# A two-layer trunk on one core: the first layer's feed-forward by pairs of chunks and seven block products, its inner width in two parts, and the keys' and queries' weights loaded by blocks

## The chip, the core and the metric

The kernel runs on one core of one Trainium2 chip. A core has a matmul engine (TensorE, "PE" in the profile), a vector engine (VectorE, "DVE"), a scalar engine (ScalarE, "ACT"), a general engine (GpSimd, "POOL") and a sync engine (SyncE, "SP") that here only starts transfers (DMAs). The engines run side by side. Each executes its own instructions in a fixed order and waits on semaphores where it needs another's result. The metric is the device time of one execution, in microseconds (us); lower is better.

## The reference

Two layers run on `x` of shape 4 x 512 x 512 (batch, tokens, width). Both branches of a layer read the same layer-normed rows:

```python
xn = _layernorm(x)
x = x + L0_attn(xn) + L0_ffn(xn)
xn = _layernorm(x)
x = x + L1_attn(xn) + L1_ffn(xn)
```

The first layer's attention is a scan. Each of 32 heads carries a 16 x 16 matrix `W1` and a bias `b1`, and goes through the 512 tokens in 32 steps of 16 tokens:

```python
def step(carry, x):
    W1_s, b1_s = carry
    xq, xk, xv, eta_mb = x
    Z1 = xk @ W1_s + b1_s
    grad = _ln_fused_l2_bwd(Z1, xv - xk, ln_w, ln_b)
    Attn1 = jnp.tril(xq @ xk.swapaxes(-1, -2))
    b1_bar = b1_s - jnp.tril(eta_mb) @ grad
    Z1_bar = xq @ W1_s - eta_mb * Attn1 @ grad + b1_bar
    last_eta = eta_mb[:, :, -1, :, None]
    W1_new = W1_s - (last_eta * xk).swapaxes(-1, -2) @ grad
    b1_new = b1_s - jnp.sum(last_eta * grad, axis=-2, keepdims=True)
    out = xq + _ln(Z1_bar, ln_w, ln_b)
    return ((W1_new, b1_new), out)
```

So a step can't begin before the step ahead of it has its gradient. The scan's output is normed again and multiplied by `o_w`.

The first layer's feed-forward has an inner width of 1408 (11 blocks of 128):

```python
g = jnp.einsum('th,ih->ti', xf, gate_w) * gate_s
u = jnp.einsum('th,ih->ti', xf, up_w) * up_s
hdn = jax.nn.silu(g) * u
out = jnp.einsum('ti,hi->th', hdn, down_w) * down_s
```

The second layer is an attention of 16 heads on low-rank latents, and a feed-forward with four experts. Everything is in 32-bit floats.

## The kernel before

**Chunks.** The first layer works on 8 chunks `ch` of 4 scan steps (64 tokens of each of the 4 batches, 256 columns). For a chunk, `norm_rows` loads and norms the rows and `norm_turn` (L154) turns them on PE into `xT`, 128 partitions by 4 blocks of the width by 256 columns. `keys` and `queries` (through `features`, L242) make `k1` and `q1` from `xT` with the weights `wk` and `wq`, which are loaded whole at the start (L163, L188) and stay on the chip. `token_tile` (L258) makes, for 128 tokens, a tile `rows` with keys, targets and learning rates, and stores it to memory by 8 small stores from SP (L294).

**The scan.** For step `n`, `prepare` (L303) loads `kv` and lays out `sk`, `km` and the query part of `wq_bd` on POOL. `first_product` (L338) is a matmul group into `pz`. `gradient` (L353 to L390) is a chain of small DVE and ACT operations on 128 x 256 elements from `pz` to `grad`. `update` (L393) copies `grad` into `g_bd` (two copies on DVE, two on ACT) and adds 16 products to the state `wacc`, which stays in PSUM. `weights_out` (L327) copies the new state to `wq_bd`, for the next `pz`. `out_operands` (L417, with `gh` on POOL, L421) and `emit_out` (L433) give the step's output in `pso`.

**Filler.** Between the parts of a step, the program calls `fill(us)`. It takes pieces from a generator `between(ch)` (L656) until the estimated lengths that the pieces yield add up to what is due: 11, 3 and 8 us in a step. `between(ch)` holds the feed-forward of chunk `ch` (`gate_up`, L465, eleven times, then `down`, L481, for each half of the chunk), the projections of the next chunk, and `finish` (L545) of the chunk before. `finish` is the norm of the scan's output, the product with `wo`, the sum of the layer and the norm for the next layer. It is itself a chain over PE, ACT and DVE: squares (`pn_sq`) into a product with `bones`, roots (`pn_rs`), a product with `onesd` for the means, another for the variances, then `wo`. The last chunks also do `latents` (L620 on), the first products of the second layer, from rows that are stored and read back (`latent_rows`).

**A gate/up block.** `gate_up(ch, i)` loads two 256 KB blocks, `wg` and `wu` (two buffers each, from SP), multiplies each with `xT` (four products of 128 x 128 by 256 columns each) into the two halves of one PSUM bank `pf` (two banks), and makes `hid` by a silu on ACT (`sg`) and one DVE operation (L478). `down` loads 11 blocks `wd` of 256 KB (four buffers, from SP) for each half of a chunk and adds 11 products of 512 columns into `pd`.

**Order.** The calls above are not the final order. The framework's planner puts the instructions of the program into one fixed order for each engine before it runs, from its own estimates of their costs and from what each needs; the queue of SP is one of these orders, and a transfer that waits for a buffer holds up those behind it. The pools give each tile name a number of buffers: a tile waits until the reader of the tile that had its buffer is done.

**Layer 1** follows from L800 on. Its four-expert feed-forward (L933 to L1018) already multiplies by seven block products where eight would be the plain way, with sums of its operands on DVE and with the partial results held on ACT. The change doesn't touch it.

Of the kernel before, what the change touches and what calls it, by code (L numbers as in the profile page):

```python
# [42 lines left out]
NI = INTER // P  # L43

# [11 lines left out]
def trunk_kernel(ctx: ExitStack, tc: tile.TileContext, a: dict, out: bass.AP):  # L56
# [49 lines left out]
    with ExitStack() as px:  # L106
# [16 lines left out]
        xTs, xns = {}, {}  # L123
# [30 lines left out]
        def norm_turn(ch):  # L154
            xTs[ch] = wk.tile([P, NC, CW], F32, tag="xT", name=f"xT{ch}", bufs=3)
            for u in range(2):
                nc.scalar.copy(xTs[ch][:, :, u * P : (u + 1) * P], transposed(xns.pop((ch, u))))
                yield 0.6
# [4 lines left out]
        wk_w = load(one, "wk", [P, NC, HS], a["wk"].rearrange("(c p) o -> p c o", p=P))  # L163
# [24 lines left out]
        wq_w = load(one, "wq", [P, NC, HS], a["wq"].rearrange("(c p) o -> p c o", p=P))  # L188
# [53 lines left out]
        def features(ch, w, got, tag, bufs):  # L242

            t = got[ch] = wk.tile([P, NC, CW], F32, tag=tag, name=f"{tag}_{ch}", bufs=bufs)
            for be in range(NC):
                pp = psum()[:, :CW]
                for c in range(NC):
                    mm(pp, w[:, c, be * P : (be + 1) * P], xTs[ch][:, c, :], c == 0, c == NC - 1)
                nc.scalar.copy(t[:, be, :], pp)
                yield 1.72  # L250

        def keys(ch):
            return features(ch, wk_w, k1, "k1", 2)

        def queries(ch):
            return features(ch, wq_w, q1, "q1", 3)
# [46 lines left out]
        def prepare(n):  # L303

            ch, i = divmod(n, CH)
            kv = wk.tile([P, B, RW], F32, tag="kv", name=f"kv_{n}", bufs=3)
# [158 lines left out]
        def gate_up(ch, i):  # L465
            if i == 0:
                hid[ch] = wk.tile([P, NI, CW], F32, tag="hid", name=f"hid_{ch}", bufs=1)
            pf = ps_ff.tile([P, 2, CW], F32, tag="pf", name=f"pf_{ch}_{i}")
            for j, nm in enumerate(("wg", "wu")):
                w = wk.tile([P, NC, P], F32, tag=nm, name=f"{nm}_{ch}_{i}")  # L470
                nc.sync.dma_start(out=w, in_=a[nm][i])
                for c in range(NC):
                    mm(pf[:, j, :], w[:, c, :], xTs[ch][:, c, :], c == 0, c == NC - 1)
            if i < 10:
                next(copies, None)
            sg = wk.tile([P, CW], F32, tag="sg", name=f"sg_{ch}_{i}")
            nc.scalar.activation(sg, pf[:, 0, :], AF.Silu, scale=gs[:, i : i + 1])  # L477
            nc.vector.scalar_tensor_tensor(  # L478
                hid[ch][:, i, :], pf[:, 1, :], us[:, i : i + 1], sg, ALU.mult, ALU.mult
            )  # L480
            yield 3.43  # L481

        def down(ch, u):
            xr = wk.tile([P, HS], F32, tag="xr", name=f"xr_{ch}_{u}")
            load_rows(xr, a["x"], ch, u)
            pd = ps_dn.tile([P, HS], F32, tag="pd", name=f"pd_{ch}_{u}")
            for i in range(NI):
                w = wk.tile([P, HS], F32, tag="wd", name=f"wd_{ch}_{u}_{i}", bufs=4)
                nc.sync.dma_start(out=w, in_=a["wd"][i * P : (i + 1) * P, :])
                mm(pd, hid[ch][:, i, u * P : (u + 1) * P], w, i == 0, i == NI - 1)  # L490
                if i in (3, 7):
                    yield 3.43
            t = wk.tile([P, HS], F32, tag="yf", name=f"yf_{ch}_{u}", bufs=4)
            nc.vector.tensor_mul(t, pd, dsc)
            nc.gpsimd.tensor_add(xr, xr, brow)
            nc.gpsimd.tensor_add(t, t, xr)
            yf[ch, u] = t
            yield 2.57
# [46 lines left out]
        def finish(ch):  # L545
# [49 lines left out]
            if ch >= NCHUNK - 2:  # L595
                t = wk.tile([P, NC, CW], F32, tag="xT", name=f"xl_{ch}", bufs=3)
                part = parts[ch] = t.rearrange("p c w -> p (c w)").rearrange("p (u c e x) -> p u c e x", u=2, c=NC, e=E)
# [10 lines left out]
        parts, lw = {}, []  # L608
# [13 lines left out]
        def latent_rows(k):  # L622
            t = parts[2 * k, 2 * k + 1] = one.tile([P, 4, NC, E, 32], F32, tag=("wk", "wv", "wq")[k], name=f"xl_{k}")
# [32 lines left out]
        def between(ch):  # L656

            fin = finish(ch - 1) if ch > 0 else iter(())
            if ch + 1 == NCHUNK:
                latent_operands()  # L660
            for i in range(NI):
                yield from gate_up(ch, i)
                if ch + 1 == NCHUNK and i in (2, 5, 8):
                    latent_rows(i // 3)
                if i == NI - 3:
                    yield from take(fin, 1)
            if ch == 0:
                yield from finish_constants()
            nxt = iter(())
            if ch + 1 < NCHUNK:  # L670
                nxt = chain(
                    norm_turn(ch + 1), keys(ch + 1), token_tile(ch + 1, 0), token_tile(ch + 1, 1), queries(ch + 1)
                )
            else:
                yield from fin
            for u in range(2):
                dn = down(ch, u)
                for j in range(3):
                    yield from take(nxt, 2)
                    yield from take(dn, 1)  # L680
                    yield from take(fin, 1)
            yield from nxt
            done.add(ch + 1)
            yield from fin
            if ch + 2 < NCHUNK:
                norm_rows(ch + 2)
            if ch + 1 == NCHUNK:
# [786 lines left out]
```

## Time and profile before

The three runs before took 2028.45, 2035.72 and 2035.77 us; the median is 2035.72. The profile is of one more execution.

| what | value |
|---|---|
| profiled execution, its own time | 2030.29 us |
| its span in the trace | 2028.3 us |
| granted clock of PE, mean | 0.998 |
| PE busy, whole span | 1968.2 us |
| layer 0 (until the first product of layer 1, `epg`) | 0 to 969.3 us |
| layer 1 | 969.3 to 2028.3 us |
| loads of `wg` and `wu` | 88 and 88, of 256 KB |
| loads of `wd` | 176, of 256 KB |

A group of instructions is printed as line, engine, operation, the tile written and the tiles read, shapes, count, busy time, mean duration in ns, and then the idle time of the engine ahead of them with what ended it. `L117` is the helper that records every matmul of layer 0, so these are told apart by their tiles. One product in 32-bit floats shows as two matmul records. The timeline gives one line for successive instructions of a kind: start, duration, engine, line, operation, tiles, shapes, count, and in brackets the idle time before it and its releaser.

### The profile page before, as it was taken

Reading aid. Unit: us, or ns where it says so; the run is one execution under the profiler, and the core shown is the slowest. Engines: PE = TensorE matmul, PEld = TensorE weight load, DVE = VectorE, ACT = ScalarE, POOL = GpSimd, SP = SyncE. Lnnn points to the kernel's source line nnn. Section 1 sums busy time; section 2 is a strip of 40 time slices with the busy share of each in tenths; the row PEclk is TensorE's granted clock in tenths of the full one; section 3 lists DMA queues with packets and bytes.
Section 4 is the critical chain, followed back from the end, with each engine's and each line's share of the span. In section 5 each row is a group of like instructions: output and inputs, shape, how many; then the busy total and the mean of one; then the engine's idle time right before and its main releaser. Section 6 shows DMA issues by size and latency. Waiting matters only on the chain.

```text
span 2028.3 us, 30787 instructions
## 1 busy us (share of the span) xinstructions
PE 1968.2 (97%) x10502; PEld 1245.2 (61%) x10502; DVE 1302.3 (64%) x2720; ACT 863.2 (43%) x1763; POOL 631.8 (31%) x707
## 2 busy tenths in 40 slices
PE   8999999999999999998999999999999999999999
PEld 6777676767676776744776445555555555555555
DVE  4546657575756574754654487777777777777773
ACT  2233343333343443422322365555555555555552
POOL 4334242434342433421001132223223232354320
PEclk9999999999999999999999999999999999999999
DMA  6757576646373655545831144344434443333332
GB/s 166 210 129 220 132 193 166 183 128 184 114 203 116 179 151 163 182 136 189 281 104 56 39 101 117 95 103 115 108 94 114 103 114 86 97 97 89 94 100 93
DMA packets 318472, 270.90 MB, mean 134 GB/s; under 512 B 87660, under 2 KB 239405, under 8 KB 317677
## 3 DMA queue, kind: packets, MB, share of 16 engines
q1 hardware_dynamic: 298080, 237.31, 43.2%
q0 software_dynamic: 8736, 26.31, 4.5%
q10 hardware_dynamic: 11500, 5.32, 0.9%
q8 instruction: 84, 1.38, 0.3%
q14 instruction: 72, 0.58, 0.1%
HBM read 174.18 MB, written 34.87 MB: 103 GB/s over the span
## 4 chain that ended last, share of the span: by engine, by line
PE 47%; DVE 1%; SPq 1%; ACT 1%; issue 0%; DMA 0%; DVEq 0%; ACTq 0%
PE sc L1134 9%; PE pc L1202 9%; PE pq L1124 7%; PE px L1245 5%; PE p L1245 4%; PE epg L969 3%; PE epo L1032 3%; PE pk L1116 2%; PE epu L969 1%; SPq L1194 1%; PE po L1302 1%; PE pw L868 1%; PE pvo L886 1%; ACT prob L1139 1%; ACT prob L1144 0%
## 5 line engine op out<-in xcount | busy, mean ns | idle before, releaser
L1139 ACT ACTIVATE prob<-sc,mx 128x512 f32<-128x512 f32 x256 | 174.3, 683 | 164.2 <-DVE mx L1136 159.4
L1134 PE MATMUL sc<-kT,qT 96*128 96x512 f32 x512 | 230.6, 592 | 1.6 <-DVE prT_head L1183 1.3
L1202 PE MATMUL pc<-prT,lv 128*128 128x512 f32 x488 | 219.6, 593 | 1.2 <-DMA prT<-tt 1.2
L1109 POOL TENSOR_TENSOR kT<-t_k,t_k 32x512 f32<-32x512 f32 x64 | 80.6, 1259 | 407.6 <-PE pq L1124 235.6
L1163 DVE STREAM_TRANSPOSE tt<-prob 128x512 f32<-128x512 f32 x248 | 170.3, 706 | 55.2 <-ACT prob L1144 43.7
L117 PE MATMUL pf<-xT,wg 128*128 128x256 f32 x704 | 173.7, 388 | 5.3 <-DMA wg<-in_wg 2.7
L1144 ACT ACTIVATE prob<-prob,sm 128x512 f32<-128x512 f32 x256 | 176.5, 713 | 0.0
L1124 PE MATMUL pq<-cq,uq 128*128 128x512 f32 x384 | 175.3, 592 | 0.8 <-ACT ctxT L1204 0.8
L1134 PEld LDWEIGHTS sc<-kT,qT 96*128 96x128 f32 x512 | 96.8, 190 | 124.1 <-issue 118.9
L1136 DVE TENSOR_REDUCE mx<-sc 128x1 f32<-128x512 f32 x256 | 168.0, 677 | 2.3 <-PE sc L1134 0.3
L117 PE MATMUL pf<-xT,wu 128*128 128x256 f32 x704 | 167.0, 380 | 1.3 <-DMA wu<-in_wu 1.3
L117 PE MATMUL pd<-wd,hid 128*128 128x512 f32 x352 | 165.9, 600 | 1.8 <-DMA wd<-in_wd 1.7
L117 PEld LDWEIGHTS pf<-xT,wg 128*128 128x128 f32 x704 | 132.1, 192 | 32.9 <-issue 7.6
L1202 PEld LDWEIGHTS pc<-prT,lv 128*128 128x128 f32 x488 | 92.5, 190 | 93.7 <-issue 90.7
L117 PEld LDWEIGHTS pf<-xT,wu 128*128 128x128 f32 x704 | 133.7, 190 | 20.4 <-DMA wu<-in_wu 2.3
L478 DVE SCALAR_TENSOR_TENSOR hid<-pf,us,sg 128x256 f32<-128x256 f32 x88 | 41.9, 477 | 153.9 <-ACT sg L477 153.5
L1124 PEld LDWEIGHTS pq<-cq,uq 128*128 128x128 f32 x384 | 72.8, 190 | 93.1 <-issue 81.5
L314 POOL TENSOR_SCALAR sk<-k,m 128x256 f32<-128x256 f32 x64 | 61.1, 964 | 179.8 <-PE pz L117 167.7
L421 POOL TENSOR_SCALAR gh<-grad,m 128x256 f32<-128x256 f32 x64 | 61.2, 967 | 153.2 <-DVE grad L390 135.5
L117 PEld LDWEIGHTS pd<-wd,hid 128*128 128x128 f32 x352 | 63.4, 190 | 60.5 <-issue 45.2
L1109 POOL TENSOR_TENSOR qT<-t_q,t_q 32x512 f32<-32x512 f32 x64 | 80.6, 1260 | 56.7 <-DVE t_q L1105 56.6
L477 ACT ACTIVATE sg<-pf,gs 128x256 f32<-128x256 f32 x88 | 41.5, 473 | 132.9 <-PE pf L117 132.5
(304 smaller groups left out, 3546.6 us busy)
## 6 DMA issues: line engine op xcount, KB each, us to landing
prT<-tt SPq DMA_DIRECT2D x992, 64.0 KB, 2.0
wd<-in_wd SPq DMA_DIRECT2D x176, 256.0 KB, 3.0
wg<-in_wg SPq DMA_DIRECT2D x88, 256.0 KB, 3.1
wu<-in_wu SPq DMA_DIRECT2D x88, 256.0 KB, 3.1
cq<-lat_d SPq DMA_DIRECT2D x48, 256.0 KB, 4.3
rows<-rows SPq DMA_DIRECT2D x128, 66.0 KB, 2.2
kv<-rows POOLq DMA_DIRECT2D x32, 264.0 KB, 4.1
gu<-in_gu SPq DMA_DIRECT2D x3, 2048.0 KB, 8.8
```

The source lines that it names most:

```text
L117: nc.tensor.matmul(out, lhsT=lhsT, rhs=rhs, start=start, stop=stop, skip_group_check=True)
L421: nc.gpsimd.tensor_scalar_mul(gh[:, :, h, :], g, m2[:, h : h + 1])
L969: nc.tensor.matmul(ps, lhsT=w[:, c, :], rhs=x[:, c], start=start and c == 0, stop=c == 1, skip_group_check=True)
L1109: nc.gpsimd.tensor_sub(t[RD:mid, :], t1[RD:mid, :], t2[RD:mid, :])
L1124: nc.tensor.matmul(pq, lhsT=w[f"uq{i}"][:, h, :], rhs=cqs[hg, b][:, i, :], start=(i == 0), stop=(i == nq - 1))
L1134: pin(nc.tensor.matmul(ps, lhsT=qT[:KQ, i * P : (i + 1) * P], rhs=kT[:KQ, :], start=True, stop=True))
L1136: pin(nc.vector.tensor_reduce(mx, ps, AX.X, ALU.max, negate=True))
L1139: pin(nc.scalar.activation(pr, ps, AF.Exp, bias=mx, scale=1.0, accum_out=sm))
L1144: pin(nc.scalar.mul(pr, pr, sm))
L1163: nc.vector.transpose(out=tt[:, :, :, i, :], in_=pr.rearrange("p (kb e j) -> p kb e j", e=2, j=K))
L1202: pin(nc.tensor.matmul(pc, lhsT=lv[:, b, k, :], rhs=prT[:, k, :], start=(k == 0), stop=(k == E - 1)))
L1245: nc.tensor.matmul(ps[:, q, :], lhsT=a[:, k, q * P : (q + 1) * P], rhs=w[:, k, :], start=start and k == 0 and q == 0, stop=k == 1, skip_gr ...
```

## The change

The first layer's feed-forward is done for a pair `k` of chunks instead of one chunk. `xT` holds both chunks of the pair. For an inner block `i`, the weights of gate and up make a 2 x 2 block matrix (gate and up, by two halves of the width 512), and the pair's `xT` another (two halves of the width, by two chunks). Their product is formed from seven block products (each two matmuls of 128 x 128 by 256 columns) instead of eight. The sums of the right-hand operand are four DVE subtractions for each pair (`right_sums`), those of the left-hand operand four POOL operations for each pair and block, one block ahead (`left_sums`). Four ACT copies and four DVE additions for each pair and block put the products together. Both `pf` banks serve one block.

`hid` holds six inner blocks of both chunks. The inner width is done in two parts, blocks 0 to 5 and 6 to 10: `down` is called twice for each half of a chunk, the first part's sums are copied from `pd` to `yf` by ACT, the second part's are added by DVE.

To make room, `wk` and `wq` no longer stay on the chip: for each chunk the four 128-wide blocks of each are loaded into the buffers of `wg` and `wu` (the first chunk's keys use `wk` loaded whole into `hid`'s buffer). `kv`, `xT` and `q1` go from three buffers to two. `between` has a new order for even and odd chunks, and the rows and the order of the latents are placed differently.

```diff
         def norm_turn(ch):
-            xTs[ch] = wk.tile([P, NC, CW], F32, tag="xT", name=f"xT{ch}", bufs=3)
+            if ch % 2 == 0:
+                xTp[ch // 2] = wk.tile([P, NC, 2, CW], F32, tag="xT", name=f"xT{ch}")
+            xTs[ch] = xTp[ch // 2][:, :, ch % 2, :]
...
-        wk_w = load(one, "wk", [P, NC, HS], a["wk"].rearrange("(c p) o -> p c o", p=P))
+        wk_w = wk.tile([P, FF_FIRST, 2, CW], F32, tag="hid", name="wk", bufs=1)
+        wk_w = wk_w[:, :NC].rearrange("p c h t -> p c (h t)")
+        nc.sync.dma_start(out=wk_w, in_=a["wk"].rearrange("(c p) o -> p c o", p=P))
...
-        wq_w = load(one, "wq", [P, NC, HS], a["wq"].rearrange("(c p) o -> p c o", p=P))
...
+        def blocks_of(nm, ch):
+            def block(be):
+                w = wk.tile([P, NC, P], F32, tag="wu" if be % 2 else "wg", name=f"{nm}_{ch}_{be}")
+                nc.sync.dma_start(
+                    out=w, in_=a[nm].rearrange("(c p) o -> p c o", p=P)[:, :, be * P : (be + 1) * P]
+                )
+                return w
+            return block
...
-            kv = wk.tile([P, B, RW], F32, tag="kv", name=f"kv_{n}", bufs=3)
+            kv = wk.tile([P, B, RW], F32, tag="kv", name=f"kv_{n}")
...
-        def gate_up(ch, i):
-            if i == 0:
-                hid[ch] = wk.tile([P, NI, CW], F32, tag="hid", name=f"hid_{ch}", bufs=1)
-            pf = ps_ff.tile([P, 2, CW], F32, tag="pf", name=f"pf_{ch}_{i}")
-            for j, nm in enumerate(("wg", "wu")):
-                w = wk.tile([P, NC, P], F32, tag=nm, name=f"{nm}_{ch}_{i}")
-                nc.sync.dma_start(out=w, in_=a[nm][i])
-                for c in range(NC):
-                    mm(pf[:, j, :], w[:, c, :], xTs[ch][:, c, :], c == 0, c == NC - 1)
...
+        def right_sums(k):
+            b11, b12, b21, b22 = (xTp[k][:, 2 * c : 2 * c + 2, h, :] for c in range(2) for h in range(2))
+            t = wk.tile([P, 4, 2, CW], F32, tag="t_sums", name=f"t_sums_{k}", bufs=1)
+            t1, t2, t3, t4 = (t[:, n] for n in range(4))
+            nc.vector.tensor_sub(t1, b12, b11)
+            nc.vector.tensor_sub(t2, b22, t1)
+            nc.vector.tensor_sub(t3, b22, b12)
+            nc.vector.tensor_sub(t4, b21, t2)
...
+        def left_sums(k, i):
+            a11, a12, a21, a22 = (w[:, 2 * c : 2 * c + 2, :] for w in lefts[k, i] for c in range(2))
+            t = wk.tile([P, 3, 2, P], F32, tag="s_sums", name=f"s_sums_{k}_{i}")
+            s1, s2, s4 = (t[:, n] for n in range(3))
+            nc.gpsimd.tensor_add(s1, a21, a22)
+            nc.gpsimd.tensor_sub(s2, s1, a11)
+            nc.gpsimd.tensor_sub(a21, a11, a21)
+            nc.gpsimd.tensor_sub(s4, a12, s2)
...
+        def gate_up(k, i):
...
+            pa = ps_ff.tile([P, 2, CW], F32, tag="pf", name=f"pfa_{k}_{i}")
+            pb = ps_ff.tile([P, 2, CW], F32, tag="pf", name=f"pfb_{k}_{i}")
+            g = wk.tile([P, 2, CW], F32, tag="cg", name=f"cg_{k}_{i}")
+            up = wk.tile([P, 2, CW], F32, tag="cu", name=f"cu_{k}_{i}", bufs=1)
+            x = pa[:, 0]
...
+            product(x, o["a11"], r["b11"], True)
+            nc.scalar.copy(g[:, 0], x)
+            product(pa[:, 1], o["a12"], r["b21"])
+            product(x, o["s2"], r["t2"])
+            nc.scalar.copy(g[:, 1], x)
+            product(pb[:, 0], o["s1"], r["t1"], True)
+            nc.scalar.copy(up[:, 1], pb[:, 0])
+            nc.vector.tensor_add(g[:, 0], pa[:, 1], g[:, 0])
             yield 3.43
+            if more:
+                left_sums(k, i + 1)
+            product(x, o["s3"], r["t3"])
+            nc.scalar.copy(up[:, 0], x)
+            product(pb[:, 0], o["s4"], r["b22"])
+            nc.vector.tensor_add(g[:, 1], pb[:, 0], g[:, 1])
+            nc.scalar.activation(g, g, AF.Silu, scale=gs[:, i : i + 1])
+            product(pb[:, 1], o["a22"], r["t4"])
+            nc.vector.tensor_add(up[:, 1], up[:, 1], up[:, 0])
+            nc.vector.tensor_add(up[:, 0], pb[:, 1], up[:, 0])
+            nc.vector.scalar_tensor_tensor(hid[k][:, n], up, us[:, i : i + 1], g, ALU.mult, ALU.mult)
+            yield 2.6
...
+        def down(ch, u, part):
...
+            parts_i = range(FF_FIRST, NI) if part else range(FF_FIRST)
...
+            if part:
+                t = yf[ch, u]
+                nc.vector.tensor_add(t, pd, t)
+                nc.vector.tensor_mul(t, t, dsc)
...
+            else:
+                t = yf[ch, u] = wk.tile([P, HS], F32, tag="yf", name=f"yf_{ch}_{u}", bufs=4)
+                nc.scalar.copy(t, pd)
...
+            if not odd:
+                yield from norm_turn(ch + 1)
+                right_sums(k)
+                for i in range(FF_FIRST):
+                    yield from gate_up(k, i)
...
+                for c in range(2):
+                    for u in range(2):
+                        if c and u:
+                            ahead(k, FF_FIRST)
+                        yield from down(ch + c, u, 0)
+                return
...
+            for i in range(FF_FIRST, NI):
+                yield from gate_up(k, i)
...
+            yield from down(ch - 1, 0, 1)
+            yield from down(ch - 1, 1, 1)
...
+                latent_rows(2)
+                for key in ((0, 1), (2, 3), 6, (4, 5)):
                     yield from latents(key)
```

## The prediction

> **What bounds the kernel now.** I read first the busy time of each engine and the forty slices, where the last layer-0 slices and the first are the ones to look at.
>
> ```profile
> PE 1968.2 (97%) x10502; PEld 1245.2 (61%) x10502; DVE 1302.3 (64%) x2720; ACT 863.2 (43%) x1763; POOL 631.8 (31%) x707
> ...
> PE   8999999999999999998999999999999999999999
> ```
>
> The matmul engine sets the time: 1968.2 of 2028.3 us. Next I cut the span into stretches (columns: stretch and length, then PE, weight loads, DVE, ACT and POOL busy, clock, DMA share, GB/s).
>
> ```profile
> 885.00:969.30 84.30, 75.88 (x324) 39.95 (x315) 37.28 (x88) 17.36 (x53) 15.11 (x24) 1.00 0.52 163
> 969.30:2028.30 1059.00, 1045.76 (x3200) 590.40 (x3199) 729.11 (x1366) 518.26 (x1082) 282.08 (x232) 1.00 0.40 104
> ```
>
> Layer 1 takes the last 1059 us. Only layer 0, the first 969.3 us, is touched. There PE is idle 46.1 us (969.3 less its busy time 923.3). So a shorter PE program is worth its whole length only where PE still has work to put behind the other waits. The timeline of PE shows those waits at the scan (columns: start, duration, engine, line, operation, count, idle before and releaser):
>
> ```profile
> 251.82 1.08 PE L117 MATMUL pz<-wq_bd,sk 128*32 128x128 f32 x32
> ...
> 257.27 1.89 PE L117 MATMUL pf<-xT,wg 128*128 128x256 f32 x8
> 258.99 1.89 PE L117 MATMUL pf<-xT,wu 128*128 128x256 f32 x8
> 263.60 0.48 PE L117 MATMUL pso<-a_bd,gh 128*32 128x68 f32 x17 [2.72 <-POOL gh L421]
> ...
> 264.69 0.70 PE L117 MATMUL pz<-gsum,bones 128*128 128x256 f32 x2
> 266.78 1.08 PE L117 MATMUL pz<-wq_bd,sk 128*32 128x128 f32 x32 [1.40 <-ACT wq_bd L332]
> ```
>
> Each of 32 scan steps runs pz on PE, then the gradient on DVE and ACT, then wacc on PE, then copies to wq_bd for the next pz. PE fills the gradient with feed-forward and projection matmuls. Summed over the stage, waits of that chain cost PE 14.5 us: g_bd 5.4, gh 5.6, wq_bd 2.5, bias_o 1.0. The feed-forward rows show the pitch: starts 257.27 and 258.99 are 1.72 apart for 4 products of 128x128 by 256 columns (two records each), 0.43 us a product.
>
> **How long the gradient is.** From DVE's timeline of a quiet step, number 11, whose pz with wq_bd began at 354.47:
>
> ```profile
> 355.62 0.42 DVE L356 TENSOR_REDUCE s<-pz 128x16 f32<-128x256 f32 x1 [0.89 <-PE pz L117]
> ...
> 363.37 0.88 DVE L395 COPY g_bd<-grad 32x256 f32<-32x256 f32 x2
> ```
>
> The first operation starts at 355.62 and g_bd is whole at 364.25: 8.6 us (8.5 to 8.9 in other quiet steps). With 0.3 from pz's end and 0.1 to wacc, PE needs 9.2 us of other work between pz and wacc; steps with other DVE work took 10 to 17. Behind wacc, wq_bd takes 2.0 us.
>
> **Part 1, two products fewer in sixteen.** Each of 44 gate/up blocks (4 pairs, 11 inner blocks) runs 7 block products of two instead of 8: 44 x 2 = 88 products x 0.4325 = **-38.0 us**. Left-hand and right-hand sums go to POOL and DVE, extra copies to ACT: POOL 176 sums of 128x256, half of this row each:
>
> ```profile
> L1235 POOL TENSOR_TENSOR s_ops<-ctxT 128x512 f32<-128x512 f32 x15 | 19.4, 1293 | 83.3 <-ACT ctxT L1204 83.3
> ```
>
> That is 0.65 x 176 = 114 us; DVE about +87 (44 blocks of four operations at 0.42 and one at 0.75 for two at 0.48, plus 16 right sums and 16 additions at 0.69); ACT about +60 us. None of the three comes near PE's total, so PE covers it everywhere outside the gradient; where that cover is missing it lengthens the chain, priced below.
>
> **Part 2, coupling inside a block.** Four products reuse one bank while ACT copies it out, both pf buffers are held by one block, and the cu buffer is single. Before shows no such block in layer 0; layer 1's seven-product feed-forward, epg, has the same shape and runs with hardly a stall (PE idle in all of layer 1: 1059 - 1046 = 13 us). That bounds it at 0 from below; above, two exposed 0.37 us copies a block, 44 x 0.8 = 35. Nearest is the epg row, but there nothing else asks ACT and DVE; I take 0.2 a block, **+9**.
>
> Here a rule is weighed. The rows first:
>
> ```profile
> L374 DVE TENSOR_TENSOR pair<-xh,by_tok x32: 361/424/1430, 54.2 to 889.5; 128x256 f32<-128x256 f32 x32
> L390 DVE TENSOR_TENSOR grad<-u,rl x32: 360/425/1304, 59.3 to 892.9; 128x256 f32<-128x256 f32 x32
> ```
>
> Minimum, median, maximum in ns: a two-input DVE operation takes 424 and at worst three times that. The Trainium skill, GPSIMD Engine Reference, Key points, says that GpSimd's SBUF interfaces are shared with VectorE and contend with DVE instructions that have two SBUF inputs. That speaks against the change: POOL's 114 us of sums are 13% of 900 us, and 7 such operations in 32 steps are 224, so about 28 collisions of 0.4 us = 11 us, half of them on the path (estimate): **+5**. By the rows' medians alone it would be 0. I take the 5; together **+14**, range 0 to 40.
>
> **Part 3, what PE has to do during the gradient.** The changed kernel's built order of instructions (it holds no times) gives the products between each pz and its wacc; I cost them by the rows above (plus 4.5%, by which layer 0's busy time exceeds my sum). Before never has under 7.5 us there. After has 4.3 in step 2, 4.2 in 7, 5.1 in 10, 1.5 in 11, 4.7 in 15, 0.6 in 19, 4.0 in 23, 0.6 in 27. The cause is in the queue: keys' and queries' weights now come as 60 loads of 256 KB on SP, into the buffers of wg and wu, so each waits there for PE to release a buffer, and down's wd loads (four buffers) stand behind them and behind the sixteen stores of rows, which wait for the token tile:
>
> ```profile
> 29.64 8.28 SPq L294 DMA_DIRECT2D rows<-rows  x16
> ...
> wd<-in_wd SPq DMA_DIRECT2D x176, 256.0 KB, 3.0
> ```
>
> 16 issues take 8.28 us, 0.52 each. So the built order puts the downs, which would have filled the gradient, behind the next wacc. Shortfalls against 9.2: 4.9 + 5.0 + 4.1 + 7.7 + 4.5 + 8.6 + 5.2 + 8.6 = 48.6, and 4.8 for other DVE operations that the order puts inside four of these gradients: 53.4. Ten other steps fall short by 0.4 to 2.9, together 12. In steps 2, 10, 19 and 23 the next pz follows wacc after 1.1 us of work where 2.0 are needed: 3.6. In three of them the products on gh come before wacc, and gh on POOL is ready about 1 us after g_bd: 3. Sum 72; before's own 14.5 go, as these waits stand in the new order's count: **+57.5**. Range: 40 (the eight alone, less 14) to 75 (busy gradients of 11).
>
> **Part 4, the tail of layer 0.** After the last step the finishing of the last chunk is a chain, of which PE covers a part:
>
> ```profile
> 922.07 1.99 PE L117 MATMUL pj<-pn_sq,bones 128*128 128x512 f32 x4 [2.88 <-ACT pn_sq L549]
> ...
> 939.71 0.59 PE L117 MATMUL pj<-pn_sq,onesd 128*128 128x256 f32 x2
> ...
> 946.37 0.50 PE L117 MATMUL pj<-onesd,pn_sq 128*128 128x1 f32 x4
> ```
>
> Behind the last wacc, before has 62.9 us of PE work and after 42, since the latents move earlier. Squares to means took 17.6 us (922.07 to 939.71), of which I count 13 for the DVE and ACT chain: after has 5.4 us of work there (7.7 short); means to variances needs 4.7 and has 0.5 (4.2); about 3 at the transposes; 15, less about 4 of before's 7.3 that go: **+11**, range 0 to 15. The 2 MB gu load now waits for the last q1 addition, with xe behind it; I find it landing 5 us ahead of its use, so 0.
>
> **Part 5, start.** The whole wq load (1 MB) is gone, but its blocks 2 and 3 queue behind the first 16 row stores: queries end near 46 us instead of 39.5, the first pz comes at the same time (47.6) with 4 us less filler behind PE: **+4**, range -2 to 8. Loads of wg and wu halve (176 to 88) and 60 new ones come, 3 us each to land behind PE's fill; a late one is bounded by the 4.0 us that PE waited for wg and wu before, and I take 0.
>
> **Edits at nothing.** kv goes from three buffers to two: its load lands in 4.1 us and its buffer is free after the step before, with whole steps (13.4 us the shortest, pz 251.29 to 264.69) between; uncovered it costs 4.1 a step. q1 and xT lose a buffer, and hid holds six blocks for two chunks: in the built order their last readers come well before the next writer; uncovered, each is one chunk's wait of a few us. On POOL four sums of 0.65 stand among sk, km and gh; one ahead of gh delays it 0.65, part of the 3 above.
>
> **Sum.** 2030.3 (the profiled execution: span 2028.3 and 2 outside) - 38.0 + 14 + 57.5 + 11 + 4 = 2078.8; I say **2079**. The runs shown are 1.8 below to 5.5 above that execution, their median 2035.7.
>
> **Rivals.** (a) *Blocks bound by ACT, DVE and the shared port.* ACT's silu, four copies and table switches stand in one queue. For it: single cu, no second pair of banks. Against: epg. At 35 us plus 1.5 us in ten more gradients, part 2 is 50: 2079 + 36 = 2115. (b) *The tail and the coupling are covered.* Parts 2 and 4 at 0: 2079 - 25 = 2054; with the smaller shortfalls of part 3 at 0 too, 2042. For it: epg; against: DVE's doubled work per block. (c) *The other side: the gradient is shorter when nothing stands beside it.* In the eight starved steps its place is DVE's sequence from pz to g_bd; each us less there saves 8. Not slower (2036) needs 2079 - 2036 = 43, so 9.2 must fall to about 3.8 there. Against: DVE's fifteen operations of the chain in the quiet step sum to 6.6 us by themselves, and 7.0 would give 2079 - 18 = 2061; so this rival keeps little chance, and that mostly where parts 2 and 4 come out low too. (d) *The change doesn't do what it says*: the built order has 88 products fewer, so no.
>
> **How the numbers follow.** As forecast 0.64, own range 2058 to 2098 (parts 2 to 5 at a mixture of their ends); (a) 0.17; (b) 0.13; (c) 0.06. Half a per cent, 10 us, is about what a measurement of this kernel can tell from no change. Below 2025.5 lies 0.05, most of (c); within, (b)'s lower half and the rest of (c), 0.09; slower 0.86. Leaving out half of (a) above 2115 and most of (c), the range is 2042 to 2115.
>
> **What the profile after would show.** PE busy near 1930 us; pf products 1232 instead of 1408 records; PE waits on g_bd of 4 to 9 us in steps 2, 7, 10, 11, 15, 19, 23 and 27, some 60 us in all; layer 1 unchanged at 1059; first epg near 1018. Part 2 is right if waits in the blocks sum to some 10 us and pair or grad stay near 424 ns in the median. The prediction fails if the starved gradients take far less than 9 us, or PE reaches those pz late, or if pf stalls are tens of us.

## The result and the profile after

The changed kernel takes 2174.7 us (median of 4 runs, 2172.35 to 2175.98) against 2035.5 us before: a ratio of 1.069, 95% interval 1.068 to 1.071. It is slower, as forecast, but by 139 us where 43 were forecast, and far above the 2115 at which the prediction's range ended.

The busy times and the forty slices of the profile after:

```profile
PE 1999.3 (92%) x10326; PEld 1230.3 (57%) x10326; DVE 1407.3 (65%) x2884; ACT 921.5 (42%) x1908; POOL 771.5 (36%) x883
...
PE   7989888788898969899789999999999999999999
...
PEclk9999999999999989999889999999999999999999
```

PE has 176 records fewer (88 products), and yet is busy 31 us longer. DVE, ACT and POOL grew by 105, 58 and 140 us, where the prediction had 87, 60 and 114. The PE row has dips through the whole first half. The clock row has dips that were not there before. The stretches (length, then busy times, clock, DMA share, GB/s) place it:

```profile
47.70:1040.00 992.30, 865.19 (x6833) 582.87 (x6832) 629.08 (x1409) 380.70 (x767) 448.14 (x584) 0.95 0.48 134
1040.00:1109.30 69.30, 50.18 (x171) 28.56 (x170) 25.08 (x54) 11.59 (x34) 12.08 (x21) 0.83 0.54 175
1109.30:2172.30 1063.00, 1047.50 (x3200) 591.35 (x3198) 729.95 (x1366) 518.15 (x1082) 281.69 (x232) 1.00 0.40 103
```

Layer 0 now ends at 1109.3 instead of 969.3. Layer 1 takes 1063 instead of 1059. In layer 0 PE's granted clock was 0.95 and, at the end, 0.83. What PE waited for in layer 0 (engine, line, releaser: total us, times, longest):

```profile
PE pso L119 <- POOL gh L440: 25.8, 7, 7.7
PE pfb L119 <- POOL s_sums L512: 18.3, 2, 9.4
PE wacc L119 <- ACT g_bd L414: 17.0, 3, 8.3
PE pj L119 <- DVE pn_sq L625: 16.5, 4, 8.7
PE pd L119 <- DMA wd<-in_wd: 8.8, 10, 2.0
PE wacc L119 <- DVE g_bd L414: 8.3, 1, 8.3
PE pz L119 <- DVE gsum L425: 7.7, 1, 7.7
PE pfa L119 <- DVE cg L544: 7.6, 4, 2.9
```

I split layer 0 of each kernel in the same way. From stretches of 1 us I add PE's busy time, its idle time, and busy time x (1 - granted clock), which is what PE lost to a lower clock; busy time less that loss is the work at full clock.

| kernel | end of layer 0 | PE idle | lost to the clock | busy at full clock |
|---|---|---|---|---|
| before | 969.3 | 46.9 | 3.3 | 919.1 |
| after | 1109.3 | 157.5 | 41.8 | 910.0 |
| before, weights by blocks (f1) | 1033.8 | 87.4 | 27.9 | 918.5 |
| after, eight products (f2) | 1058.3 | 108.5 | 26.1 | 923.7 |
| after, merged stores (g1) | 1061.7 | 111.1 | 39.2 | 911.4 |
| the same, eight products (g2) | 1005.9 | 69.3 | 11.7 | 924.9 |
| f1 with merged stores (g3) | 982.9 | 52.2 | 8.3 | 922.4 |
| before, merged stores (g4) | 965.9 | 43.8 | 3.4 | 918.6 |
| g1, no left sums, no copies (h3) | 1007.8 | 88.5 | 24.7 | 894.6 |

After against before: idle +110.6, clock +38.5, work at full clock -9.1, layer 1 +4: 144 us, the difference of the two spans (2172.3 - 2028.3).

### The profile page after: what moved, and what is told of

Read it like the earlier page. It is cut to its first block, busy times and chain, and to the rows that moved or that the text cites. A ratio compares the mean times of both kernels' runs of the same rounds, so it can differ in the third digit from the quotient of the medians.

```text
span 2172.3 us, 31148 instructions
## 1 busy us (share of the span) xinstructions
PE 1999.3 (92%) x10326; PEld 1230.3 (57%) x10326; DVE 1407.3 (65%) x2884; ACT 921.5 (42%) x1908; POOL 771.5 (36%) x883
## 3 DMA queue, kind: packets, MB, share of 16 engines
q1 hardware_dynamic: 316560, 228.92, 39.2%
## 4 chain that ended last, share of the span: by engine, by line
PE 74%; DVE 13%; DMA 4%; ACT 3%; issue 2%; POOL 2%; SPq 1%; ACTq 0%; DVEq 0%; POOLq 0%
PE pj L119 12%; PE sc L1260 9%; PE pc L1328 9%; PE pq L1250 7%; PE pfa L119 5%; PE px L1371 5%; PE pd L119 4%; PE pfb L119 4%; PE p L1371 4%; PE epg L1095 3%; PE epo L1158 3%; PE pk L1242 2%; PE pz L119 2%; PE epu L1095 1%; DMA wd<-in_wd 1%
## 5 line engine op out<-in xcount | busy, mean ns | idle before, releaser
L119 PE MATMUL pd<-wd,hid 128*128 128x512 f32 x352 | 178.8, 626 | 20.4 <-DMA wd<-in_wd 8.8
L119 PE MATMUL pfa<-xT,wg 128*128 128x256 f32 x352 | 95.2, 393 | 3.6 <-ACT cg L538 3.1
L1254 ACT ACTIVATE qT<-pq,b_UQ 64x512 f32<-64x512 f32 x64 | 43.6, 682 | 110.0 <-PE pq L1250 110.0
L544 DVE TENSOR_TENSOR cg<-pfa,cg 128x256 f32<-128x256 f32 x44 | 18.2, 414 | 109.8 <-ACT cg L541 109.3
L340 POOL TENSOR_SCALAR km<-kv,m2n 128x256 f32<-128x256 f32 x64 | 62.8, 992 | 74.8 <-PE wacc L119 62.6
L1225 DVE SCALAR_TENSOR_TENSOR t_k<-pk,b_UK,trig_k 32x512 f32<-32x512 f32 x64 | 47.9, 748 | 63.1 <-ACT kT L1243 63.0
L1225 DVE SCALAR_TENSOR_TENSOR t_q<-pq,b_UQ,trig_q 32x512 f32<-32x512 f32 x64 | 47.9, 748 | 60.1 <-ACT qT L1254 58.5
```

The lines of the kernel that those rows point to most:

```text
L119: nc.tensor.matmul(out, lhsT=lhsT, rhs=rhs, start=start, stop=stop, skip_group_check=True)
L1225: nc.vector.scalar_tensor_tensor(t1[RD:mid, :], ps[RD:mid, :], bias[RD:mid, :], trig[RD:mid, :], ALU.add, ALU.mult)
```

## The experiments

Theory A said that the starved gradients come from SyncE's queue; B, from the blocks of keys' and queries' weights; C, that an idle spell costs clock afterwards; D, that the seven products' coupling costs. Before took 2033 to 2035.5 us (medians) beside each set of runs.

**e1, the stores of rows from ScalarE's queue.**

```diff
-                    nc.sync.dma_start(
+                    nc.scalar.dma_start(
                         out=rows_d[ch][i, ...
```

> The changed kernel with one edit: the 128 stores of rows are started from ScalarE's queue instead of SyncE's. Theory A (in SyncE's queue the wd loads stand behind the rows stores, so the built order has no feed-forward for the gradients at the ends of chunks): PE's work between pz and wacc, by the built order, is 8.1 us or more in every step instead of 0.6 to 5.1 in eight of them, so the waits of 5 to 9 us in the scan go (about 70 us of idle time) and with them some ten spells of half clock at 2 us each: about 2085 us (2065 to 2105). Theory B (the wd loads stand behind the blocks of keys' and queries' weights): nothing changes, 2174. If idle spells have no price of their own beside their length: about 2105.

2184.2 us, ratio 1.075 (1.072 to 1.078): a little slower than the changed kernel. The built order did have 8 us or more of PE work in every gradient, yet idle time was 161.7 us. The view of the tile `rows` tells why (count: minimum, median, maximum ns; then who waited for it, in us and times):

```profile
L313 ACTq DMA_DIRECT2D rows<-rows x128: 309/441/2427, 32.3 to 926.4; - x128
...
  ACT q L255: 50.8, 6
  ACT rows L289: 25.9, 5
  ACT rows L309: 15.2, 5
```

The 128 issues, at a median of 0.44 us, and the waits of the stores themselves held ScalarE: behind them the copies of queries alone waited 50.8 us. The edit put a new wait in the place of the old one; it neither supports nor refutes A.

**e2, the block loads from ScalarE's queue.**

```diff
-                nc.sync.dma_start(
+                nc.scalar.dma_start(
                     out=w, in_=a[nm].rearrange("(c p) o -> p c o", p=P)[:, :, be * P : (be + 1) * P]
```

> The changed kernel with one edit: the 60 block loads of wk and wq are started from ScalarE's queue instead of SyncE's. Theory A: the starved steps stay, 2170 to 2180. Theory B: they go, about 2085 to 2105.

2175.0 us, one run: unchanged, and in its profile PE idles between pz and wacc as long in the starved steps as in the changed kernel's (8.4 us in steps 11 and 27). The queue of the block loads is not what starves the gradients.

**e3 and i1, zero products in the starved steps.**

```diff
+        idle_w = one.tile([P, 32], F32, tag="idle_w", name="idle_w")
+        nc.gpsimd.memset(idle_w, 0.0)
+        extra = {2: 14, 7: 12, 10: 14, 11: 18, 15: 14, 19: 20, 23: 14, 27: 20}
         def update(n, g, pre):
+            for _ in range(extra.get(n, 0)):
+                mm(wacc[:32].rearrange("p b be d -> p (b be d)"), idle_w, wvl[:, 0, :CW], False, True)
```

> The changed kernel with 126 added products of a zero weight tile (128 rows by 32 columns) with 256 columns, added into the state, in the eight starved steps only (12 to 20 a step): 54 us of PE work that changes no value. Theory C (an idle spell of PE over 3 us halves its clock, and each such spell costs 2 us more afterwards): idle time of layer 0 falls by about 55 us, about ten of 21 half-clock spells go, and the kernel is faster by 15 to 20 us, 2155 to 2160, with more work. If the clock has no part in it: the gradient chain sets the time in these steps and the kernel stays at 2174, or it is slower where a step's products last longer than its chain, up to 2185.

2169.0 us (2166.6 to 2174.3), 6 us below the changed kernel with 54 us more of PE work. In its profile idle time is 110.8 us (-47) and the loss to the clock 25.2 (-16.6), as C has it; busy time grew by 39, and the sum is -8. The whole gain is under half of what C foretold, and the runs of the two kernels overlap. i1 has 91 such products instead of 126:

> As the run with zero products (126 of them, 54 us of work, 2169 us; its profile had 39 us more busy time, 47 us less idle time and 17 us less lost to the half clock than the changed kernel), with 91 of them (39 us), so that no step's work outlasts its gradient chain. Theory C (an idle spell has a price after it): the zero products only take the place of idle time, and the spells they end leave 10 to 16 us: 2158 to 2164. If the clock's price is nothing: 2174.

2186.1 us (2175.5 to 2190.9): slower than the changed kernel, against both numbers. Its built order differs elsewhere too; idle time fell only to 131.1 and the loss to the clock stayed at 41.8, with a wait of 8.8 us in another step (3). So the clock's price is seen in the traces, but no run isolates it as a total, and every edit brings another planned order with it.

**f1, weights by blocks alone, on the kernel before.**

```diff
-        wq_w = load(one, "wq", [P, NC, HS], a["wq"].rearrange("(c p) o -> p c o", p=P))
...
-                    mm(pp, w[:, c, be * P : (be + 1) * P], xTs[ch][:, c, :], c == 0, c == NC - 1)
+                    mm(pp, wb[:, c, :], xTs[ch][:, c, :], c == 0, c == NC - 1)
```

> The kernel before with one part of the change alone: keys' and queries' weights by blocks (60 loads into the buffers of wg and wu, the first keys' weights whole in hid's buffer), everything else as before, eight products. If blocks starve the gradients by themselves: by its built order PE has 0.6, 2.3 and 2.5 us of work between pz and wacc in steps 3, 7 and 28, short by 8.6, 6.9 and 6.7 us, with three half-clock spells of 2 us and 4 us at the start: +32, about 2066. If the loads are hidden: 2035.

2095.3 us, ratio 1.031 (1.027 to 1.034): +62, where +32 was expected. This one part costs almost half of the loss. Its timeline in step 3, PE first and then SyncE's queue:

```profile
147.68 0.63 PE L117 MATMUL pso<-wq_bd,wh 128*32 128x64 f32 x32
158.35 0.32 PE L117 MATMUL pso<-a_bd,gh 128*32 128x68 f32 x1 [10.05 <-POOL gh L434]
...
162.10 2.86 PE L117 MATMUL pf<-xT,wg 128*128 128x256 f32 x8
```

```profile
142.17 0.37 SPq L484 DMA_DIRECT2D wg<-in_wg  x1
142.64 0.38 SPq L484 DMA_DIRECT2D wu<-in_wu  x1
143.53 0.33 SPq L484 DMA_DIRECT2D wg<-in_wg  x1
```

PE sits idle for 10 us (148.3 to 158.4) and only behind the update of the state takes a gate product. Its `wg` block had been started at 143.53 at the latest and taken 3.2 us to land. The load was in time. It is PE's fixed order, made from the planner's estimates, that has the product behind the gradient. The price is beyond the step as well: 162.10 to 164.80 is 2.7 us for a group that takes 1.72 at full clock.

**f2, eight products in the changed kernel.**

```diff
-            product(x, o["a11"], r["b11"], True)
-            nc.scalar.copy(g[:, 0], x)
...
+            for ps, wb, half in ((pa, w[0], False), (pb, w[1], True)):
+                for h in range(2):
+                    for c in range(NC):
+                        mm(ps[:, h], wb[:, c, :], xTp[k][:, c, h, :], c == 0, c == NC - 1)
...
```

> The changed kernel with eight block products for seven and no sums, copies or additions of products; pairs, two parts, weights by blocks and the order of the pieces stay. If the seven products cost more by their coupling than they take off PE, as between the two runs with the rows stores on ScalarE (66 us): 2105 to 2115. If that was peculiar to those two: 38 us of work more and nothing gained, 2190 to 2210.

2112.5 us, ratio 1.039 (1.036 to 1.043). With more PE work the kernel is 62 us faster: seven products cost 62 us here. Pairs, two parts and the new order cost 17 beyond f1. The steps from before to f1, to f2 and to after (62 + 17 + 62 = 141) make up the whole loss. e4, the same in e1's frame, agrees (2118.3 against 2184.2):

> As the run with the rows stores on ScalarE's queue, and with eight block products in place of seven: pairs of chunks, inner width in two parts and the weights by blocks stay, the sums of operands and the copies and additions of products are gone. If the 88 products taken out are worth their 38 us: 38 us above that run. If the split into products in two banks with copies gives most of that back, as PE's records of layer 0 suggest (29 us more busy time at full clock than 88 products fewer would leave): 5 to 15 us above it. If the coupling costs more than it brings: below it.

**f3 and f4, the left-hand sums.** f3 makes all four on VectorE (the first is shown), f4 leaves them out.

```diff
-            nc.gpsimd.tensor_add(s1, a21, a22)
+            nc.vector.tensor_add(s1, a21, a22)
...
```

> The changed kernel with the left-hand sums on VectorE instead of GpSimd. If the sums are late because they stand in GpSimd's queue behind the load of kv and km (18.3 us of waits on s_sums in two steps, with two half-clock spells): 2150 to 2160. If these steps are starved whoever makes the sums: 2170 to 2185, with the waits under another name.

> The changed kernel without the left-hand sums (seven products of the plain weight blocks, so the gated products are other numbers): the products, copies, additions and order stay. If GpSimd's 176 sums and the shared interface are what costs: down by 30 us or more, to 2140 or less. If the coupling through PSUM, the copies and the starved gradients are: 2160 to 2175.

f3: 2162.3 us, between its two cases; the waits of 9.8 and 8.2 us in steps 7 and 15 stay under VectorE's name. f4: 2150.1 us, also between its cases: the sums cost 25 us.

**g1 to g4, 32 stores of rows instead of 128, on the same queue.**

```diff
-        rows_d = [dram.tile([CH, NS, K, B, RW], ...
+        rows_d = [dram.tile([CH, K, NS, B, RW], ...
-                for i in range(CH):
-                    p0 = b2 * CT + i * K
-                    nc.sync.dma_start(
-                        out=rows_d[ch][i, :, :, 2 * u + b2, :].rearrange("s t x -> t s x"), in_=t[p0 : p0 + K]
-                    )
+                nc.sync.dma_start(
+                    out=rows_d[ch][:, :, :, 2 * u + b2, :].rearrange("i t s x -> (i t) s x"),
+                    in_=t[b2 * CT : (b2 + 1) * CT],
+                )
-            nc.gpsimd.dma_start(out=kv, in_=rows_d[ch][i].rearrange("s t b x -> (s t) b x"))
+            nc.gpsimd.dma_start(out=kv, in_=rows_d[ch][i].rearrange("t s b x -> s t b x"))
```

> The changed kernel with the 128 stores of rows merged into 32, on the same queue (a store for each batch of a token tile, memory laid out by token first, kv read accordingly). Theory A, second form (the stores fill SyncE's queue in the plan, so the plan puts feed-forward behind gradients, whether its loads have landed on the chip or not): in the new built order PE has 7.5 us or more between pz and wacc in every step, so about 65 us of idle time and 20 us of half clock go: 2085 to 2100. Theory D (what costs is the coupling of products, copies and sums inside the gate/up blocks): 2150 to 2175.

2124.2 us, ratio 1.044 (1.041 to 1.047): 50 us below the changed kernel, between the numbers of the two theories (24 above A's, 26 below D's). In layer 0, PE's waits of more than 5 us fall from ten to two, and neither is in the scan. So the starved gradients were worth about 50 us; something else holds the rest.

> The same with eight products in place of seven, without sums, copies and additions. Theory A: the seven products' price was in the starved gradients, so with these filled the 14 us of busy time at full clock that they save stand: 10 to 15 us above the run with merged stores. Theory D: the coupling stays, and this one is 30 us or more below it.

2071.4 us (1.018; 1.015 to 1.020). Seven products cost 53 us also where every gradient has its filler: theory D. This is where g1 waits (timeline of PE, one block beside a gradient):

```profile
311.51 0.67 PE L119 MATMUL pfb<-xT,s_sums 128*128 128x256 f32 x2 [0.55 <-ACT cu L542]
314.87 1.13 PE L119 MATMUL pfa<-t_sums,wu 128*128 128x256 f32 x4 [2.68 <-DVE cg L543]
315.83 0.75 PE L119 MATMUL pfb<-xT,s_sums 128*128 128x256 f32 x2
316.51 0.42 PE L119 MATMUL wacc<-g_bd,km 128*32 128x64 f32 x2
316.87 2.08 PE L119 MATMUL pfa<-xT,wg 128*128 128x256 f32 x4
```

PE's next product into the bank waits 2.68 us for the block's addition on VectorE, which stands in line with a gradient's operations. wacc, which ends that gradient, is next but one behind it on PE. Then a group of four records takes 1.87 us (316.87 to the next at 318.74) where it takes 0.86 at full clock.

The line on VectorE is also slower there. Its operations, and then those of GpSimd beside them:

```profile
309.29 0.83 DVE L392 TENSOR_TENSOR pair<-xh,by_tok 128x256 f32<-128x256 f32 x1
310.15 0.83 DVE L397 TENSOR_TENSOR pair<-pair,kv 128x256 f32<-128x256 f32 x1
311.02 0.83 DVE L398 TENSOR_TENSOR pair<-pair,xh 128x256 f32<-128x256 f32 x1
...
312.95 0.42 DVE L405 TENSOR_TENSOR xh<-xh,s 128x256 f32<-128x256 f32 x1
```

```profile
308.92 0.91 POOL L512 TENSOR_TENSOR s_sums<-s_sums,wg 128x256 f32<-128x256 f32 x1
309.80 0.91 POOL L513 TENSOR_TENSOR wu<-wg,wu 128x256 f32<-128x256 f32 x1
310.66 0.91 POOL L514 TENSOR_TENSOR s_sums<-wg,s_sums 128x256 f32<-128x256 f32 x1
```

While GpSimd makes the left-hand sums, a two-input operation of the gradient takes 0.83 us instead of 0.42. Over the whole of g1's layer 0, 97 such operations with nothing on GpSimd beside them took 419 ns in the mean, and 30 that had a left-hand sum beside them for more than half of their usual time took 833.

> The kernel before with keys' and queries' weights by blocks (2095 us with the stores as they were) and the rows stores merged. Theory A: its three starved gradients are filled in the built order, 2035 to 2055. If the blocks cost by holding the buffers of wg and wu: 2080 to 2095.

2041.6 us (1.003; 1.001 to 1.004). Of f1's 62 us, 54 go with nothing changed but the stores of `rows` and their layout, although the load of `kv` takes longer in the new layout (6.2 us instead of 3.7, medians of g3 and f1).

> The kernel before with the rows stores merged alone. It has no gradient under 7.5 us of work: about 2033, or a few us below it where its waits on g_bd and gh (11 us) shrink; above 2040 only if the larger stores are slower to land.

2027.5 us (2025.5 to 2032.5), ratio 0.997 (0.996 to 0.998): the lowest of all, 0.3% below the kernel before. Weights by blocks cost 14 us over it.

**h1 to h4, what is in the seven products' price.** All have merged stores. h2 leaves the copies and additions out:

```diff
-            nc.scalar.copy(g[:, 0], x)
...
-            nc.scalar.copy(g[:, 1], x)
...
-            nc.vector.tensor_add(g[:, 1], pb[:, 0], g[:, 1])
-            nc.scalar.activation(g, g, AF.Silu, scale=gs[:, i : i + 1])
+            nc.scalar.activation(g, pa, AF.Silu, scale=gs[:, i : i + 1])
...
```

> The changed kernel with merged rows stores (2124 us) and without the left-hand sums (the products take the plain weight blocks, so the gated products are other numbers). If the sums' price is their place in GpSimd's queue, as in the run without them on the unmerged kernel (25 us): about 2100. If that was only a change of starved steps: 2115 to 2125.

> The changed kernel with merged rows stores, with all sums and all seven products, but without the four copies and four additions that put the products together (silu and the last operation read the banks directly, so the gated products are other numbers). If the coupling of PE with ACT and DVE inside a block costs what is left of the seven products' price (53 + 38 - 25 = 66 us): about 2060. If the many short products cost by themselves, or the tail of layer 0: 2090 or more.

> The changed kernel with merged rows stores, seven products, right-hand sums, and neither left-hand sums nor copies and additions. If sums and copies are all of the price: the eight-product kernel less the 38 us of products, 2071 - 38 = 2033. If short products or the thinner tail keep a part of it: 2045 or more.

> The changed kernel with merged rows stores and the left-hand sums on VectorE (a whole kernel, nothing left out). If GpSimd's queue is what makes the sums dear: near the run without sums, about 2105. If VectorE, on which the gradient runs, pays for 74 us more of work: 2115 to 2135.

Without sums 2093.3 (-31), without copies and additions 2101.9 (-22), without both 2080.5 (-44), sums on VectorE 2121.4 (-3, within the spread of the runs). h1 went below its first case; h2, h3 and h4 met their second. So copies and additions are not the greater part; the sums weigh about as much or more (the runs of h1 and h2 overlap). With merged stores VectorE is no better home for the sums than GpSimd. Without both the kernel still stands 47 us above the 2033 expected, and 9 above the eight products of g2. Against g2 the profile of h3 shows work at full clock -30.3, idle +19.2, clock +13.0 and layer 1 longer by 11.7. About 10 of the idle time and several us of the clock are the tail of layer 0:

```profile
961.36 2.97 PE L119 MATMUL pj<-pn_sq,bones 128*128 128x512 f32 x4 [2.89 <-ACT pn_sq L616]
977.14 1.19 PE L119 MATMUL pj<-pn_sq,onesd 128*128 128x256 f32 x2 [8.67 <-DVE pn_sq L609]
982.50 0.99 PE L119 MATMUL pj<-onesd,pn_sq 128*128 128x1 f32 x4 [4.17 <-DVE pn_sq L609]
996.69 1.11 PE L146 MATMUL pj<-ident,x 128*128 128x128 f32 x4 [2.73 <-DVE x L141]
```

The waits of the last 60 us of layer 0 add up to 19.1 us here, 9.3 in g2. The longer start of layer 1 (one wait of 7.8 us on PE, whose named releaser had long been done) was not tried further, nor was the order of the tail; why is open.

## Why the prediction missed

The sign was right, and PE's waits came where they were forecast. The size was a third: the step that failed most is part 2, the cost of putting the products together, and the clock was left out of the sum.

**Part 3, the starved gradients: right in place, near in size.** The eight steps named hold eight of the nine longest single waits of PE in the scan: 6.0, 9.4, 5.1, 8.3, 8.9, 8.4, 7.7 and 8.4 us in steps 2, 7, 10, 11, 15, 19, 23 and 27, together 62 where 53 were worked out. In step 27:

```profile
895.93 0.63 PE L119 MATMUL pso<-wq_bd,wh 128*32 128x64 f32 x32
904.90 1.08 PE L119 MATMUL wacc<-g_bd,km 128*32 128x64 f32 x32 [8.35 <-ACT g_bd L414]
...
908.18 4.37 PE L119 MATMUL pd<-wd,hid 128*128 128x512 f32 x8
```

```profile
890.37 3.85 SPq L568 DMA_DIRECT2D wd<-in_wd  x4
```

From the first operation on pz to g_bd took 8.7 us there, as counted. Two things were missed. In steps 7 and 15 PE waits for left sums that stand in GpSimd's queue behind `sk`, the copies to `wq_bd`, the load of `kv` and `km`; that these two were on the list is in part luck. In step 24, the ninth, the first product of the next pz stands ahead of the filler and waits 7.7 us for gsum, where I had counted work only up to wacc. Of the two reasons given, the stores of rows are one (merging them is worth 50 us), and the place of the block loads in SyncE's queue is not (e2, one run). They work through the plan, as the prediction has it: on the chip the first of the wd loads above was started at 890.37 and landed 2.5 us later, before the wait began. PE idled beside landed weights. The same holds for the first down product behind the wait in steps 10, 11 and 19, and within 0.2 us in step 2 (loads and products matched in order).

**Part 2, coupling and sums: the term that was mis-sized most.** "Nearest is the epg row ... I take 0.2 a block", 9 us and 5 for the port, is the step that failed. Seven products cost 53 to 66 us more than eight in three frames, that is 91 to 104 with the 38 us of products that they take off. In the epg row no gradient asks VectorE and ScalarE; the prediction said so, and took that row's price all the same. In layer 0 they run the gradient, so a block's addition waits for its turn, PE waits for the addition, and wacc waits on PE behind it. The upper bound of 40 was too low as well: it priced a copy's own length, and not the queue in front of it.

The table splits the 102 us between the profiles of g1 and g2 (64, and the 38 us of products): idle time +41.8, clock +27.5, layer 1 +8.3, and 24.5 of the 38 that don't show as less work. Of the idle time, 24 are waits of PE inside the blocks (26.5 us against 2.3; in the kernel after they are 34.1, of which 18.3 for the left sums of steps 7 and 15; the prediction's own sign for part 2 was some 10), and 10 are the tail. Without sums, copies and additions (h3) the kernel gets 44 of the 91 back. The other 47, with the tail and layer 1's start among them, stay even then, and their cause is open.

The port is in these numbers. By the median of `pair`, 424 before and 426 after, nothing happened; by the operations beside a left-hand sum the rule that the prediction weighed holds (g1 above). Over their medians the gradient's operations of 128 x 256 lost 15.9 us in the kernel after, against 7.3 before, and 23.4 in g1 against 4.2 in g2. The 11 us of collisions were about right; how much of them reaches the time no run isolates.

**Part 1: 38 us of products are not 38 us.** With neither sums nor copies 30.3 of the 38 show (894.6 in h3 against 924.9 in g2, at full clock). With both, 13.5 (911.4). The copies and additions are what hides them: with the sums alone it is 894.2 (h2), with copies and additions alone 907.6 (h1). PE's records count the rest as busy, perhaps as short waits within the block (an inference from the difference).

**A term that the sum did not have: the clock.** "88 products x 0.4325" and every other product were priced at the clock of before, 0.998. The windows of PE in step 7 (busy, clock, DMA share, GB/s):

```profile
276.00:278.00 2.00, 2.00 (x66) 1.00 0.95 270
278.00:280.00 2.00, 0.28 (x2) 1.00 0.93 354
280.00:282.00 2.00, 0.00 (x0) 0.92 0.82 309
282.00:284.00 2.00, 0.00 (x0) 0.50 0.51 135
...
286.00:288.00 2.00, 0.33 (x1) 0.50 0.25 44
288.00:290.00 2.00, 2.00 (x6) 0.50 0.24 91
290.00:292.00 2.00, 2.00 (x6) 0.52 0.26 26
292.00:294.00 2.00, 1.90 (x25) 1.00 0.77 248
```

After some 3.5 us of idleness the granted clock is 0.50, and it stays there for about 4 us of work: 2.1 us lost after a wait of 9.4. Layer 0 has 21 such spells, 41.8 us, against two and 3.3 us before, where no wait after the first was over 3.1 us. The Trainium skill states this in TensorE: Matmul & The Clock Gate, Part 1: idle for a window of about 3.4 us, and the gate passes half of the pulses until a similar window was busy. The traces agree on the length and not on "idle" (last section). The trace before has only two cases of it, and the prediction gave it no price; with eight waits of 4 to 9 us forecast, it belonged in the sum at about 2 us each (41.8 us by 21), an estimate of 16 us, and more for the tail.

**Parts 4 and 5.** The tail's waits (the last 60 us of layer 0) went from 7.3 to 19.1 us, +11.8 against +11; its half clock (7.4 us) and 4 us at layer 1's start were not in it. At the start the first operation on pz came at 57.5 instead of 49.4, not at the same time as I had it, and PE was busy 45.7 of the first 60 us instead of 49.9. That 4.2 stands against the 4 forecast is luck.

Put together, the prediction's idle time (57.5 + 14 + 11 + 4 = 86.5) came to 110.6; its saving of 38 to 9.1; the clock, at nothing, to 38.5; layer 1, at nothing, to 4. (PE's busy time in layer 0 before, 923.3 in the prediction, is 922.4 by the windows, so idle time there is 46.9 and not 46.1; nothing hangs on it.) Rival (a), blocks bound by ACT, DVE and the shared port, was the right one to fear, and at 2115 was still too cheap. Rival (c), a shorter gradient, had nothing in it: 8.7 us in the quiet starved steps 2, 10, 19 and 27.

## What to carry to other kernels

Price a finer split of matmuls by who puts the pieces together: where these engines also run a chain that the matmuls wait for, the pieces queue behind it, and the row of a stage without such a chain is no guide. A stall of the matmul engine that takes most of a stretch of some 3.4 us has a second price in its clock, about 2 us each here, which belongs in the sum. And where a planner fixes the order beforehand, a transfer's place in its plan can starve an engine although the data has landed: count the issues that a queue is planned for, and merge them.

## What was not expected of the hardware

It is not the length of a wait that costs the clock. In all nineteen traces of this case the clock records change only at marks 3.41 us apart, and the marks don't follow the kernel: they lie elsewhere in each trace. What counts is how busy PE was from one mark to the next. Of 11,199 such stretches at full clock, 199 had PE busy for less than 0.40 of the stretch (1.4 us), and each was followed by half clock. None with more than 0.66 (2.2 us) was; in between there are both. First g1, then the kernel before, from mark to mark (stretch, length, PE busy, clock, DMA share, GB/s):

```profile
749.63:753.05 3.42, 1.36 (x6) 1.00 0.52 173
753.05:756.46 3.41, 3.38 (x8) 0.50 0.00 0
```

```profile
50.24:53.66 3.42, 1.03 (x6) 1.00 0.30 47
53.66:57.07 3.41, 3.41 (x9) 0.50 0.53 159
...
917.23:920.64 3.41, 1.95 (x5) 1.00 1.04 411
920.64:924.06 3.42, 1.99 (x5) 1.00 1.03 397
924.06:927.47 3.41, 3.41 (x8) 1.00 1.07 389
```

A wait of 2.0 us in g1 (until 751.89) and one of 2.4 us before (until 53.20) each fall within one stretch, and half clock follows. The wait of 2.9 us ahead of 922.07 is split by a mark, and the clock stays full. So g1, with only two waits over 5 us, has 18 spells at half clock, 39.2 us. For a prediction the place of the marks is not known; a wait of 2 to 3 us may cost a spell, and one of 4.1 us or more costs one wherever the marks lie, since the larger half of it takes 0.60 of a stretch (an estimate from these numbers).
